# A three-stage transformer block on one core: the last stage's first row is normalised in attention buffers, its chunks start earlier, and VectorE takes more of the clamps

## The chip, the core and the metric

The kernel runs on one core of a Trainium2 chip. TensorE (PE) multiplies matrices and writes them to PSUM, VectorE (DVE) and ScalarE (ACT) work elementwise and can read PSUM, GpSimd (POOL) works on SBUF, and SyncE (SP) issues most of the DMAs. All DMAs that SP issues go through one queue, those of ACT through another. The metric is the device time of one execution in microseconds (us).

## What is computed

The input is 8 rows of 512 tokens by 512 numbers. Three stages follow each other, each with a residual:

```python
x = x + 0.5 * ffn(layernorm(x), w_gate_up, w_proj)      # stage a
x = x + attention(layernorm(x), Wq, Wk, Wv, Wo)          # stage b: 32 heads of 16, window 128
x = x + 0.5 * ffn(layernorm(x), w_gate_up, w_proj)      # stage c, the same weights

def ffn(x):                       # weights are ternary by groups of 64, times a group's scale
    gate, up = split(x @ quant(w_gate_up).T)             # 2 x 2048 columns
    h = silu(gate) * up
    return rms_norm(h) @ quant(w_proj).T                 # 2048 -> 512
```

## The kernel before, in words

**Feed-forward stages.** A row's 2048 hidden columns are 16 chunks of 128. To keep precision, what is multiplied is split in a high and a low term (`xs[:, 0]` and `xs[:, 1]`, `hs[:, 0]` and `hs[:, 1]`). One chunk (`chunk`, `gate_or_up`, L297) is 16 matmuls for gate and up, a silu on ACT, a product on DVE (L313) and squares on POOL for the norm (L583 to L587). The down projection of a chunk (`project`, L330) is 8 matmuls and needs both terms of h (high on ACT L318, low on DVE L322). A layernorm (`norm`) has three parts for each of a row's 4 blocks of 128 tokens: statistics (DVE, L206, L207), scaling (DVE, L219) and transposition (PE, L227, then ACT and, when split, DVE, L230 and L231). Tiles for weights of one chunk hold 512 KB and are loaded again in stage c from a copy in DRAM (`weights_loaded`, L255).

**Attention.** It goes in 128 units u: 8 rows times 4 groups of heads (i = u // 4) times 4 token blocks (t = u % 4). PE, DVE, ACT, POOL and SP all run in the order in which the loop issues work (`manual_schedule`), so a wait on one engine holds everything after it there. In unit u PE makes the transposed scores (`probabilities`, tile `sp`, L921), the weighted values of unit u-1 (`weighted`, `av`, L956), the scores for the maxima of unit u+6 (`maxima`, `sm`, L873), at t = 2 a small transposition (`neg`, L900), and then one filler of 8 matmuls (L797): values `wv` of the next row at t = 0, an output projection `wo` at t = 1, queries `wq` at t = 2 and keys `wk` at t = 3, both for i+3. The scores of a unit are clamped (ACT L933 for three of four groups, DVE L929 for one), go through an exponential (ACT L935) and two selects (POOL L940). Silu and the exponential need different ACT tables, and each change is an `ACT_TABLE_LOAD` of 1.28 us. Queries and keys are copied to a ring by SP's DMAs (L828, L840) out of the tiles `raw` (`q_31` and `k_31` are the last). The denominators go to DRAM and back (L979, L989), are inverted on DVE (`inverted`, L993, at t = 2 of the next group of units), stored (L994), spread by eight DMAs (L1001) and multiplied in by POOL (L1007), all in the order of the queue.

**The close.** From unit 116 on there are no more queries and keys, and from 112 on no values: fillers run out. The first row of stage c is therefore worked off beside the last units (`FirstRow`, called `row_c`). `closing` is unit 112. There the right-hand buffers of the attention's begin are freed (`right`: the x, normalised x and transposed x of row 0 and even rows, `wv`, and the values `vones0`), and stage c's own buffers are put there. The row's norm is made in units 113 to 116, chunk c in unit 117 + c, and its down projection in units 133 to 148. Chunk weights are loaded where buffers come free: chunk 0 at unit 112, chunks 1 to 8 at unit 116 (in place of `raw`, `wq`, `wk` and `xs1`), 9 to 11 at 120, 12 to 14 at 124, and 15 at 129, followed there by eight loads of the projection's weights (L639, 512 KB each). In memory, the tile of chunk 1's weights lies over the end of `q_31` and the first 1216 bytes (a partition) of `k_31`, and a load waits until all that read the old tiles under it are done. The products h of chunks 0 to 12 are stored to DRAM (L652) and read back (`back`, L658) for the down projection; those of the last KEPT = 3 stay. The output projections of row 7 come in units 138 to 141.

Places in the trace: a unit begins with the first `sp` matmul. Unit 112 begins at 1561.83 us, the keys of unit 115 (the last) end at 1593.62, unit 118 begins at 1612.42, unit 128 at 1685.20, and the chunks of stage c's second row begin at 1764.20. From there on PE works without a pause to the end.

The lines that place the norm, the chunks and the loads:

```python
closing, early = units - row, units - row + TB + 1
for u in range(-3 * TB, early + 2 * FC):
    if u == closing:
        right.close()
        row_c.opened(ps_s, ps_av, ps_mm)
        row_c.weights(range(1))
    if u == closing + TB:
        brought.close()
        row_c.weights(range(1, 9))
    ...
    if 0 <= u - early < FC:
        row_c.chunk(u - early)
    if 0 <= u - early - FC < FC:
        row_c.down(u - early - FC)
```

Of the kernel before, what the change touches and what calls it, by code (L numbers as in the profile page):

```python
# [24 lines left out]
def macaron_block(  # L25
# [166 lines left out]

    def norm(xnpool, xspool, psum, tag, xt, split, name, each=False):

        if split:
            xs = xspool.tile([P, 2, DC, T], F32R, tag="xs", name=f"xs_{name}")
        else:
            xs = xspool.tile([P, DC, T], F32, tag="xs", name=f"xs_{name}")  # L200
        mv = small.tile([P, TB, 2], F32, tag="mv", name=f"mv_{name}")
        rstd = small.tile([P, TB], F32, tag="nrstd", name=f"rstd_{name}")

        def statistics(t):
            st = small.tile([P, 6], F32, tag="st", name=f"st_{name}_{t}")
            nc.vector.bn_stats(st, xt[:, t, :])  # L206
            nc.vector.bn_aggr(mv[:, t, :], st)  # L207

            if each or t == TB - 1:
                which = slice(t if each else 0, t + 1)  # L210
                var = small.tile([P, TB], F32, tag="nvar", name=f"var_{name}_{t}")
                nc.vector.tensor_scalar(var[:, which], mv[:, which, 1], LN_EPS, None, ALU.add)
                inv_sqrt(rstd[:, which], var[:, which])

        xns = {}

        def scaled(t):
            xns[t] = xnpool.tile([P, D], F32, tag="xn", name=f"xn_{name}_{t}")
            nc.vector.tensor_scalar(  # L219
                xns[t], xt[:, t, :], mv[:, t, 0:1], rstd[:, t : t + 1], ALU.subtract, ALU.mult  # L220
            )

        def transposed(t):
            xn = xns.pop(t)
            pt = psum.tile([P, DC, P], F32, tag=tag, name=f"ptn_{name}_{t}")
            for c in range(DC):
                nc.tensor.transpose(pt[:, c, :], xn[:, c * P : (c + 1) * P], ident)  # L227
            cols = slice(t * P, (t + 1) * P)
            if split:
                nc.scalar.copy(xs[:, 0, :, cols], pt)  # L230
                nc.vector.tensor_tensor(  # L231
                    xs[:, 1, :, cols], pt, xs[:, 0, :, cols].bitcast(F32), ALU.subtract
                )
            else:
                nc.scalar.copy(xs[:, :, cols], pt)

        return xs, statistics, scaled, transposed
# [4 lines left out]
    def ffn_stage(kind, source, target, first):  # L242
# [27 lines left out]
        if first:  # L270
            xspools.append(pool(s, f"xs0_{kind}", 1))
# [4 lines left out]
            xspools.append(pool(s, f"xs1_{kind}", 1))  # L276
# [16 lines left out]
        def gate_or_up(b, c, i):  # L293
            ps = bank("mm", [P, T], f"gu_{kind}{b}_{c}_{i}")
            for k in range(DC):
                for part in range(2):
                    nc.tensor.matmul(  # L297
                        ps, wgu[c][:, i * DC + k, :], xss[b][:, part, k, :],
                        start=(k == 0 and part == 0), stop=(k == DC - 1 and part == 1),
                    )  # L300
# [309 lines left out]
        class FirstRow:  # L610


            KEPT = 3

            def opened(self, ps_s, ps_av, ps_mm):
                nonlocal xnpool, work
                banks["mm"] = banks["acc"] = banks["tr"] = ps_s, "s"
                banks["ms"] = ps_mm, "mm"
                self.ps_av = ps_av
                xspools.append(pool(s, f"xs0_{kind}", 1, side="right"))  # L620
                xpools.append(pool(s, f"x0_{kind}", 1, side="right"))
                xnpool = pool(s, f"xn_{kind}", 2, side="right")
                work = pool(s, f"work_{kind}", 5, side="right")
                self.kept, self.terms = {}, {}
                row_loaded(0)
                self.norm = norms[0]

            def weights(self, chunks):
                weights_made(pool(s, f"weights{chunks[0]}_{kind}", 1, side="right"), chunks)
                weights_loaded(chunks)  # L630

# [23 lines left out]
            def back(self, e):  # L655
                if e < FC - self.KEPT:
                    self.kept[e] = work_tile("back", 0, e)
                    nc.sync.dma_start(self.kept[e], h_kept[e])  # L658

            def down(self, n):  # L660
                order = [*range(FC - self.KEPT, FC), *range(FC - self.KEPT)]
                if n == 0:
                    self.ops = outputs(0)
                    banks["tr"] = self.ps_av, "av"
                    for e in range(self.KEPT):
                        self.back(e)
                if n >= 1 and n + 2 < FC:
                    ahead = order[n + 2]
                    self.terms[ahead] = high_term(0, ahead, self.kept[ahead])
                    low_term(self.kept.pop(ahead), self.terms[ahead])  # L670
                    self.back(ahead + self.KEPT)
                project(self.ops, order[n], self.terms.pop(order[n]), order[0], order[-1])
# [18 lines left out]
        def rest():  # L691
            xspools.append(pool(s, f"xs1_{kind}", 1))
            banks_opened()
# [9 lines left out]
    def attention_begun(step, ps_tr):  # L703

        at = 3
        if step == at:
# [4 lines left out]
            nc.sync.dma_start(xt, rows_a[0])  # L711
            begun["norm"] = norm(begun["xn"], begun["xs0"], *ps_tr, xt, False, "b0")
        for part, first_step in enumerate((at + 3, at + 8, at + 9)):
# [3 lines left out]
    def attention_stage(row_c):  # L717
# [11 lines left out]
        xpool, xnpool = begun["x"], begun["xn"]  # L729
        fixed = {name: pool(right, f"{name}_b", 1, side="right") for name in ("wv", "vones0")}  # L730
        fixed["wo"] = pool(base, "wo_b", 1)
# [9 lines left out]
        for name in ("wq", "wk"):  # L741
            fixed[name] = pool(brought, f"{name}_b", 1)
        xspools = [begun["xs0"], pool(brought, "xs1_b", 1)]

# [13 lines left out]
        for name, src in (("wq", wq_t), ("wk", wk_t), ("wv", wv_t), ("wo", wo_t)):  # L758
            attn_w[name] = fixed[name].tile([P, DC, D], F32, name=f"{name}_sb")
            if name != "wo":  # L760
# [39 lines left out]
        def project(w, b, j, done):  # L800
            cols = slice(j * P, (j + 1) * P)
            pairs = [(attn_w[w][:, k, cols], xss[b][:, k, :]) for k in range(DC)]
            sum_of_products(f"{w}_{b}_{j}", pairs, done)
# [40 lines left out]
        def values(b, t):  # L844
            rows = slice(t * P, (t + 1) * P)
            pairs = [(xss[b][:, k, rows], attn_w["wv"][:, k, :]) for k in range(DC)]

# [58 lines left out]
        def probabilities(u):  # L906
# [19 lines left out]
            for g in range(NG):  # L926
                under = pT[:, 2 * g : 2 * g + 2, : n * P]
                if g == 1:
                    nc.vector.tensor_scalar(  # L929
# [99 lines left out]
        }  # L1029
        s.enter_context(tc.manual_schedule(engines=engines))  # L1030
        outputs = {}
        for out_b in range(B):
            for out_t in range(TB):
                at = TB * (NJ * (out_b + 1) + 2 + out_t) + 1
                outputs[at if out_b < B - 1 else units + 2 * TB + 2 + out_t] = out_b, out_t
        closing, early = units - row, units - row + TB + 1
        for u in range(-3 * TB, early + 2 * FC):
            i, t = u // TB, u % TB
            b, j = i // NJ, i % NJ
            if u == closing:  # L1040
                right.close()
                row_c.opened(ps_s, ps_av, ps_mm)
                row_c.weights(range(1))
# [6 lines left out]
            if u == closing + 3 * TB:  # L1050
                rings[0].close()
                row_c.weights(range(12, 15))
            if u == units + 1:
                scores.close()
                row_c.weights(range(15, FC))
                row_c.down_opened()
            if 0 <= u < units:
                probabilities(u)
# [55 lines left out]
        base.close()  # L1114

    ffn_stage("a", lambda b: tokens(x, b), lambda b: rows_a[b], True)
    row_c, rest = ffn_stage("c", lambda b: rows_b[b], lambda b: tokens(out, b), False)
    attention_stage(row_c)
    rest()


# [26 lines left out]
```

## Time and profile before

| | us |
|---|---|
| median of 3 runs | 2405.08 |
| lowest, highest | 2404.55, 2410.36 |
| the profiled execution: its own time | 2405.92 |
| its span | 2404.2 |
| PE busy in the span | 2333.5 (97%) |
| the close, unit 112 to the second row's chunks (1561.83 to 1764.20) | 202.4 |
| of it PE busy | 188.1 |

The profiled execution is 1.7 us longer than its span (what lies around it) and 0.8 us above the median. A line of the timeline gives the start, the duration, engine, line of code, operation, output and inputs, and how often it came in a row; in brackets stands how long the engine had been idle and whom it waited for. "PEclk" or the column PEclk is the granted TensorE clock as a share of full speed. SPq and ACTq are DMA issues; their duration is that of the issuing, not of the transfer.

### The profile page before, as it was taken

Reading aid. Unit: us, or ns where it says so; the run is one execution under the profiler, and the core shown is the slowest. Engines: PE = TensorE matmul, PEld = TensorE weight load, DVE = VectorE, ACT = ScalarE, POOL = GpSimd, SP = SyncE. Lnnn points to the kernel's source line nnn. Section 1 sums busy time; section 2 is a strip of 40 time slices with the busy share of each in tenths; the row PEclk is TensorE's granted clock in tenths of the full one; section 3 lists DMA queues with packets and bytes.
Section 4 is the critical chain, followed back from the end, with each engine's and each line's share of the span. In section 5 each row is a group of like instructions: output and inputs, shape, how many; then the busy total and the mean of one; then the engine's idle time right before and its main releaser. Section 6 shows DMA issues by size and latency. Waiting matters only on the chain.

```text
span 2404.2 us, 42982 instructions
## 1 busy us (share of the span) xinstructions
PE 2333.5 (97%) x16824; PEld 1721.1 (72%) x16824; DVE 1301.7 (54%) x3673; ACT 987.0 (41%) x1432; POOL 902.4 (38%) x746
## 2 busy tenths in 40 slices
PE   5999999999999999999999999989999999999998
PEld 4778888888888555555555555556688888888886
DVE  7884544444543566767667676663254444444443
ACT  6773222222222156655666666558222222222221
POOL 0000345444445223433333333335334544544544
PEclk9899999999999999999999999989999999999999
DMA  4443200000001334344444443453610010010000
GB/s 163 143 150 135 84 20 16 35 19 17 36 35 36 105 71 113 87 125 121 110 127 108 118 113 104 102 181 125 211 62 18 18 36 18 18 36 18 18 18 18
DMA packets 89995, 185.78 MB, mean 77 GB/s; under 512 B 22464, under 2 KB 26560, under 8 KB 86720
## 3 DMA queue, kind: packets, MB, share of 16 engines
q1 hardware_dynamic: 74480, 141.87, 20.9%
q10 hardware_dynamic: 15312, 41.16, 4.6%
q8 instruction: 132, 2.16, 0.4%
q14 instruction: 71, 0.58, 0.1%
HBM read 78.64 MB, written 45.61 MB: 52 GB/s over the span
## 4 chain that ended last, share of the span: by engine, by line
PE 88%; DVE 4%; ACT 3%; DMA 2%; issue 1%; POOL 1%; SPq 0%; ACTq 0%; POOLq 0%; DVEq 0%
PE gu_c L297 18%; PE gu_a L297 18%; PE o_c L330 9%; PE o_a L330 9%; PE wv L797 5%; PE wq L797 5%; PE wk L797 5%; PE wo L797 5%; PE av L956 4%; PE sp L921 4%; PE sm L873 4%; PE neg L900 1%; ACT pT L935 1%; PE ptn_a L227 1%; PE ptn_b L227 1%
## 5 line engine op out<-in xcount | busy, mean ns | idle before, releaser
L297 PE MATMUL gu_a<-xs_a,wgu_a 128*128 128x512 f32 x2048 | 497.0, 396 | 8.0 <-ACT sg_a L308 3.0
L297 PE MATMUL gu_c<-xs_c,wgu_c 128*128 128x512 f32 x2048 | 491.9, 393 | 0.4 <-ACT sg_c L308 0.4
L297 PEld LDWEIGHTS gu_a<-xs_a,wgu_a 128*128 128x128 f32 x2048 | 385.6, 190 | 91.3 <-ACT sg_a L308 4.3
L940 POOL TENSOR_SCALAR_AFFINE_SELECT pT<-pT 128x1024 f32<-128x1024 f32 x224 | 243.2, 1106 | 528.9 <-ACT pT L935 524.8
L297 PEld LDWEIGHTS gu_c<-xs_c,wgu_c 128*128 128x128 f32 x2048 | 381.8, 188 | 83.2 <-issue 2.3
L881 DVE CUSTOM_DVE_ANT_0 seen<-sm,window 128x256 f32<-128x256 f32 (+1 forms) x1024 | 331.4, 387 | 84.2 <-PE sm L873 83.5
L330 PE MATMUL o_c<-wp_c,hs_c 128*128 128x512 f32 x1024 | 256.8, 395 | 4.1 <-ACT hs_c L318 3.5
L330 PE MATMUL o_a<-wp_a,hs_a 128*128 128x512 f32 x1024 | 257.1, 396 | 1.6 <-DVE hs_a L322 1.6
L313 DVE TENSOR_TENSOR h_c<-gu_c,sg_c 128x512 f32<-128x512 f32 x128 | 88.3, 690 | 287.6 <-PE gu_c L297 251.6
L586 POOL TENSOR_TENSOR sq_c<-h_c 128x512 f32<-128x512 f32 x120 | 125.1, 1042 | 302.1 <-DVE h_c L313 290.9
L933 ACT ACTIVATE pT<-sp 128x512 f32<-128x512 f32 (+1 forms) x384 | 181.2, 545 | 134.7 <-PE sp L921 134.7
L330 PEld LDWEIGHTS o_c<-wp_c,hs_c 128*128 128x128 f32 x1024 | 192.8, 189 | 48.5 <-ACT hs_c L318 4.0
L330 PEld LDWEIGHTS o_a<-wp_a,hs_a 128*128 128x128 f32 x1024 | 193.0, 190 | 42.0 <-DVE hs_a L322 2.5
L935 ACT ACTIVATE pT<-pT 128x2048 f32<-128x2048 f32 (+1 forms) x128 | 217.4, 1699 | 8.4 <-DVE neg_terms L891 3.1
L313 DVE TENSOR_TENSOR h_a<-gu_a,sg_a 128x512 f32<-128x512 f32 x128 | 88.3, 690 | 231.1 <-PE gu_a L297 226.4
L587 POOL TENSOR_TENSOR ss_c<-ss_c,sq_c 128x512 f32<-128x512 f32 x120 | 188.7, 1573 | 9.0
L586 POOL TENSOR_TENSOR sq_a<-h_a 128x512 f32<-128x512 f32 x90 | 94.2, 1047 | 225.2 <-DVE h_a L313 214.5
L308 ACT ACTIVATE sg_c<-gu_c 128x512 f32<-128x512 f32 x128 | 76.6, 598 | 248.7 <-PE gu_c L297 239.0
L318 ACT CAST hs_c<-h_c 128x512 fp32r<-128x512 f32 x115 | 71.4, 621 | 233.6 <-DVE h_c L313 233.6
L308 ACT ACTIVATE sg_a<-gu_a 128x512 f32<-128x512 f32 x128 | 76.4, 597 | 206.3 <-PE gu_a L297 201.9
L318 ACT CAST hs_a<-h_a 128x512 fp32r<-128x512 f32 x115 | 71.4, 620 | 207.5 <-DVE h_a L313 205.1
L322 DVE TENSOR_TENSOR hs_c<-h_c,hs_c 128x512 fp32r<-128x512 f32 x115 | 112.7, 980 | 75.0 <-ACT hs_c L318 75.0
(134 smaller groups left out, 3023.1 us busy)
## 6 DMA issues: line engine op xcount, KB each, us to landing
ks<-k SPq DMA_DIRECT2D x128, 256.0 KB
qs<-q SPq DMA_DIRECT2D x128, 128.0 KB
wf_gu<-w_gate_up_dram SPq DMA_DIRECT2D x16, 512.0 KB
wgu_kept<-wgu_a ACTq DMA_DIRECT2D x16, 512.0 KB
rows_a<-x_a ACTq DMA_DIRECT2D x8, 1024.0 KB
x_b<-rows_a SPq DMA_DIRECT2D x8, 1024.0 KB
oT<-sums SPq DMA_DIRECT2D x64, 128.0 KB
rep<-inverses SPq DMA_DIRECT2D x256, 32.0 KB
```

What stands on the lines that cost most here:

```text
L297: nc.tensor.matmul(ps, wgu[c][:, i * DC + k, :], xss[b][:, part, k, :], start=(k == 0 and part == 0), stop=(k == DC - 1 and part == 1),)
L308: nc.scalar.activation(sg, gate, AF.Silu)
L313: nc.vector.tensor_tensor(h, up, sg, ALU.mult)
L318: nc.scalar.copy(hs[:, 0, :], h)
L330: nc.tensor.matmul(ops[t], hs[:, part, t * P : (t + 1) * P], wp[e // 2][:, e % 2, :], start=(e == begin and part == 0), stop=(e == end and ...
L586: nc.gpsimd.tensor_tensor(sq, h, h, ALU.mult)
L587: nc.gpsimd.tensor_tensor(sumsq, sumsq, sq, ALU.add)
L797: nc.tensor.matmul(ps, lhs, rhs, start=(n == 0), stop=(n == len(pairs) - 1))
L881: nc.vector.tensor_tensor_reduce(out=seen[:, : n * P], in0=tiles[g][:, h, : n * P], in1=window[:, (2 - n) * P :], scale=-1.0, scalar=3.4e3 ...
L933: nc.scalar.activation(under, tiles[g][:, :, : n * P], AF.Relu, scale=-1.0)
L935: nc.scalar.activation(seen, seen, AF.Exp, scale=-1.0)
L940: nc.gpsimd.affine_select(out=half, in_=half, compare_op=ALU.is_ge, fill=0.0, base=0, pattern=[[0, 2 * NG], [sign, P]], channel_multiplier ...
```

## The change

- The norm of stage c's row 0 moves from units 113 to 116 to the attention's row 6: the row is loaded at unit 96, statistics are made at units 98, 100, 102 and 104, scaling at 107 to 110, transposition at 108 to 111. It uses the attention's x buffer, its normalised-x buffers, and for the two terms the buffers of `xs0` and `wv`, which are therefore kept to the very end; at unit 112 only `vones0` is freed, for the work tiles and chunk 0's weights.
- Chunk 0 moves from unit 117 to 113, chunk c (1 to 15) from 117 + c to 115 + c. The output projection that was in unit 113 goes to 112. The down projection goes from units 133 to 148 to units 131 to 146.
- Chunk weights are loaded two a unit instead of all at once where their buffers come free. Chunk 1's load stays in unit 116, where now chunk 1 is too. Chunk 15's stays in unit 129.
- KEPT is 2 instead of 3, so chunk 13's product too goes to DRAM and back. The first three reads back are issued in units 129, 130 and 131 instead of all in the first down step, and the high and low terms are made two steps ahead from the first step on.
- In the last six units, 122 to 127, DVE makes the clamps of three groups and ACT that of one.

```diff
-    def norm(xnpool, xspool, psum, tag, xt, split, name, each=False):
-        if split:
-            xs = xspool.tile([P, 2, DC, T], F32R, tag="xs", name=f"xs_{name}")
-        else:
-            xs = xspool.tile([P, DC, T], F32, tag="xs", name=f"xs_{name}")
+    def norm(xnpool, xspools, psum, tag, xt, split, name, each=False):
+        xs = [
+            p.tile([P, DC, T], F32R if split else F32, tag="xs", name=f"xs{n}_{name}")
+            for n, p in enumerate(xspools)
+        ]
...
         class FirstRow:
-            KEPT = 3
-            def opened(self, ps_s, ps_av, ps_mm):
-                nonlocal xnpool, work
+            KEPT = 2
+            def opened(self, ps_s, ps_av, ps_mm, xpool, xn, terms):
+                nonlocal xnpool
...
-                xspools.append(pool(s, f"xs0_{kind}", 1, side="right"))
-                xpools.append(pool(s, f"x0_{kind}", 1, side="right"))
-                xnpool = pool(s, f"xn_{kind}", 2, side="right")
-                work = pool(s, f"work_{kind}", 5, side="right")
+                xspools.append(terms)
+                xpools.append(xpool)
+                xnpool = xn
                 self.kept, self.terms = {}, {}
                 row_loaded(0)
                 self.norm = norms[0]
+                self.coming = []
+
+            def working(self):
+                nonlocal work
+                work = pool(s, f"work_{kind}", 5, side="right")
 
             def weights(self, chunks):
                 weights_made(pool(s, f"weights{chunks[0]}_{kind}", 1, side="right"), chunks)
-                weights_loaded(chunks)
+                self.coming += chunks
+
+            def load(self):
+                if self.coming:
+                    weights_loaded([self.coming.pop(0)])
...
                 if n == 0:
                     self.ops = outputs(0)
                     banks["tr"] = self.ps_av, "av"
-                    for e in range(self.KEPT):
-                        self.back(e)
-                if n >= 1 and n + 2 < FC:
-                    ahead = order[n + 2]
-                    self.terms[ahead] = high_term(0, ahead, self.kept[ahead])
-                    low_term(self.kept.pop(ahead), self.terms[ahead])
-                    self.back(ahead + self.KEPT)
+                if n + 2 < FC:
+                    self.terms[n] = high_term(0, n, self.kept[n])
+                    low_term(self.kept.pop(n), self.terms[n])
+                    self.back(n + 3)
...
-                if g == 1:
+                if g == 1 or (g > 1 and u >= units - AHEAD):
                     nc.vector.tensor_scalar(
                         under, tiles[g][:, :, : n * P], -1.0, 0.0, ALU.mult, ALU.max
                     )
...
+        closing = units - row
...
                 at = TB * (NJ * (out_b + 1) + 2 + out_t) + 1
+                if at == closing + 1:
+                    at = closing
                 outputs[at if out_b < B - 1 else units + 2 * TB + 2 + out_t] = out_b, out_t
-        closing, early = units - row, units - row + TB + 1
-        for u in range(-3 * TB, early + 2 * FC):
+        chunk_at = {closing + 1: 0, **{closing + TB + c: c + 1 for c in range(FC - 1)}}
+        down_at = closing + TB + FC - 1
+        for u in range(-3 * TB, down_at + FC):
+            if u == closing - row:
+                row_c.opened(ps_s, ps_av, ps_mm, xpool, xnpool, [begun["xs0"], fixed["wv"]])
             if u == closing:
-                right.close()
-                row_c.opened(ps_s, ps_av, ps_mm)
+                first_values.close()
+                row_c.working()
                 row_c.weights(range(1))
...
             if u == closing + 3 * TB:
                 rings[0].close()
-                row_c.weights(range(12, 15))
+                row_c.weights(range(12, FC - 1))
             if u == units + 1:
                 scores.close()
-                row_c.weights(range(15, FC))
+                row_c.weights(range(FC - 1, FC))
+                row_c.load()
                 row_c.down_opened()
+            if closing <= u < units:
+                row_c.load()
+                row_c.load()
...
-            for part, first in enumerate((1, 2, 3)):
+            for part, first_step in enumerate((closing - row + 2, closing - 5, closing - 4)):
                 for block in range(TB):
-                    if u == closing + first + (0 if part == 0 else block // 2):
+                    if u == first_step + block * (2 if part == 0 else 1):
                         row_c.norm[part](block)
-            if 0 <= u - early < FC:
-                row_c.chunk(u - early)
-            if 0 <= u - early - FC < FC:
-                row_c.down(u - early - FC)
+            if down_at - 2 <= u < down_at + 1:
+                row_c.back(u - down_at + 2)
+            if u in chunk_at:
+                row_c.chunk(chunk_at[u])
+            if u >= down_at:
+                row_c.down(u - down_at)
```

More of the change, by code (lines that the diff above doesn't have):

```diff
@@ L229, in transposed @@
             if split:
-                nc.scalar.copy(xs[:, 0, :, cols], pt)
+                nc.scalar.copy(xs[0][:, :, cols], pt)
                 nc.vector.tensor_tensor(
-                    xs[:, 1, :, cols], pt, xs[:, 0, :, cols].bitcast(F32), ALU.subtract
+                    xs[1][:, :, cols], pt, xs[0][:, :, cols].bitcast(F32), ALU.subtract
                 )
             else:
-                nc.scalar.copy(xs[:, :, cols], pt)
+                nc.scalar.copy(xs[0][:, :, cols], pt)
         return xs, statistics, scaled, transposed
@@ L270, in ffn_stage @@
         if first:
-            xspools.append(pool(s, f"xs0_{kind}", 1))
+            xspools.append(2 * [pool(s, f"xs0_{kind}", 2)])
             xpools += 2 * [pool(s, f"x_{kind}", 2)]
@@ L275, in ffn_stage @@
             weights_made(pool(s, f"weights1_{kind}", 1), range(EARLY, FC))
-            xspools.append(pool(s, f"xs1_{kind}", 1))
+            xspools.append(2 * [pool(s, f"xs1_{kind}", 2)])
             projection_made(pool(s, f"weights2_{kind}", 1))
@@ L297, in gate_or_up @@
                     nc.tensor.matmul(
-                        ps, wgu[c][:, i * DC + k, :], xss[b][:, part, k, :],
+                        ps, wgu[c][:, i * DC + k, :], xss[b][part][:, k, :],
                         start=(k == 0 and part == 0), stop=(k == DC - 1 and part == 1),
@@ L655, in back @@
             def back(self, e):
-                if e < FC - self.KEPT:
+                if e < FC - self.KEPT and e not in self.kept:
                     self.kept[e] = work_tile("back", 0, e)
@@ L691, in rest @@
         def rest():
-            xspools.append(pool(s, f"xs1_{kind}", 1))
+            xspools.append(2 * [pool(s, f"xs1_{kind}", 2)])
             banks_opened()
@@ L711, in attention_begun @@
             nc.sync.dma_start(xt, rows_a[0])
-            begun["norm"] = norm(begun["xn"], begun["xs0"], *ps_tr, xt, False, "b0")
+            begun["norm"] = norm(begun["xn"], [begun["xs0"]], *ps_tr, xt, False, "b0")
         for part, first_step in enumerate((at + 3, at + 8, at + 9)):
@@ L729, in attention_stage @@
         xpool, xnpool = begun["x"], begun["xn"]
-        fixed = {name: pool(right, f"{name}_b", 1, side="right") for name in ("wv", "vones0")}
+        first_values = ExitStack()
+        fixed = {"wv": pool(right, "wv_b", 1, side="right")}
+        fixed["vones0"] = pool(first_values, "vones0_b", 1, side="right")
         fixed["wo"] = pool(base, "wo_b", 1)
@@ L742, in attention_stage @@
             fixed[name] = pool(brought, f"{name}_b", 1)
-        xspools = [begun["xs0"], pool(brought, "xs1_b", 1)]
+        xspools = [[begun["xs0"]], [pool(brought, "xs1_b", 1)]]
         s = ExitStack()
@@ L758, in attention_stage @@
         for name, src in (("wq", wq_t), ("wk", wk_t), ("wv", wv_t), ("wo", wo_t)):
-            attn_w[name] = fixed[name].tile([P, DC, D], F32, name=f"{name}_sb")
+            attn_w[name] = fixed[name].tile([P, DC, D], F32, tag="xs", name=f"{name}_sb")
             if name != "wo":
@@ L801, in project @@
             cols = slice(j * P, (j + 1) * P)
-            pairs = [(attn_w[w][:, k, cols], xss[b][:, k, :]) for k in range(DC)]
+            pairs = [(attn_w[w][:, k, cols], xss[b][0][:, k, :]) for k in range(DC)]
             sum_of_products(f"{w}_{b}_{j}", pairs, done)
@@ L845, in values @@
             rows = slice(t * P, (t + 1) * P)
-            pairs = [(xss[b][:, k, rows], attn_w["wv"][:, k, :]) for k in range(DC)]
+            pairs = [(xss[b][0][:, k, rows], attn_w["wv"][:, k, :]) for k in range(DC)]
             def kept(ps):
@@ L1114, in attention_stage @@
         base.close()
+        return right
     ffn_stage("a", lambda b: tokens(x, b), lambda b: rows_a[b], True)
     row_c, rest = ffn_stage("c", lambda b: rows_b[b], lambda b: tokens(out, b), False)
-    attention_stage(row_c)
+    right = attention_stage(row_c)
     rest()
+    right.close()
 def kernel(L0_attn_x, L0_attn_Wq, L0_attn_Wk, L0_attn_Wv, L0_attn_Wo, L0_ffn_w_gate_up, L0_ffn_w_proj):
```

## The prediction

> **What bounds the kernel now.** I read the page's busy times and slices first, then a table by stages, then the timelines of PE, SP, DVE and ACT in the close, and last the waits of the DMA queue.
>
> The page: PE is busy 97% of the span, so only its idle or slow time can be won. Between start and end one slice alone falls short in PE and in clock, the 27th (1563 to 1623), where the close begins.
>
> ```profile
> PE 2333.5 (97%) x16824; PEld 1721.1 (72%) x16824; DVE 1301.7 (54%) x3673; ACT 987.0 (41%) x1432; POOL 902.4 (38%) x746
> PE   5999999999999999999999999989999999999998
> PEclk9899999999999999999999999989999999999999
> ```
>
> Stages (from:to, length, busy PE, PEld, DVE, ACT, POOL, clock, DMA share, GB/s): the attention before the close, units 112 to 115, 116 and 117, 118 to 127, and the rest of the close. In the first PE has no pause. Then 4.6, 1.3, 3.8 and 4.5 us are idle, and the granted clock falls to 0.84 and 0.91.
>
> ```profile
> 1541.00:1561.83 20.83, 20.83 (x233) 11.52 (x231) 13.38 (x68) 11.17 (x17) 8.75 (x8) 1.00 0.41 112
> 1561.83:1593.62 31.79, 27.18 (x303) 15.86 (x303) 19.56 (x87) 15.08 (x21) 9.74 (x9) 0.84 0.48 136
> 1593.62:1612.42 18.80, 17.46 (x169) 11.61 (x167) 11.60 (x42) 11.87 (x16) 4.27 (x4) 0.91 0.75 240
> 1612.42:1685.20 72.78, 68.95 (x777) 50.84 (x776) 27.74 (x97) 63.49 (x76) 43.20 (x39) 1.00 0.40 136
> 1685.20:1764.20 79.00, 74.51 (x314) 52.30 (x314) 28.62 (x49) 16.91 (x28) 20.07 (x17) 0.98 0.54 176
> ```
>
> PE's timeline: what follows a pause is slow. The same eight matmuls of 512 columns take 3.60 us at full clock, 6.05 after a pause of 2.73, and the projection's 8 take 3.83 after 3.53, where 32 in a row take 7.70, or 1.925 for 8.
>
> ```profile
> 1579.71 1.09 PE L900 MATMUL neg<-ident,neg_terms 128*128 128x128 f32 x4 [2.73 <-DVE neg_terms L892]
> 1580.59 6.05 PE L797 MATMUL wq<-xs_b,wq_sb 128*128 128x512 f32 x8
> 1708.53 3.60 PE L797 MATMUL wo<-wo_sb,oT 128*128 128x512 f32 x8
> 1716.65 1.88 PE L330 MATMUL o_c<-wp_c,hs_c 128*128 128x512 f32 x7 [0.61 <-DVE hs_c L322]
> 1722.06 3.83 PE L330 MATMUL o_c<-wp_c,hs_c 128*128 128x512 f32 x8 [3.53 <-ACT hs_c L318]
> ```
>
> SP's timeline and its wait: the copies of the last keys are issued to 1598.20, and the first weights load over their source waits 4.8 us for them to land. Later, one weights load and eight of the projection stand in the queue ahead of the denominators' way back.
>
> ```profile
> 1595.06 3.14 SPq L840 DMA_DIRECT2D ks<-k  x4
> 1603.12 4.19 SPq L255 DMA_DIRECT2D wgu_c<-wgu_kept  x8
> 1693.40 0.35 SPq L255 DMA_DIRECT2D wgu_c<-wgu_kept  x1
> 1693.86 4.63 SPq L639 DMA_DIRECT2D wp_c<-wp_kept  x8
> 1699.03 0.32 SPq L989 DMA_DIRECT2D den<-dens  x1
> 1717.65 3.26 SPq L658 DMA_DIRECT2D back_c<-h_kept  x5
> ```
> ```profile
> SPq L255 <- DMA ks<-k: 4.8, 1, 4.8
> ```
>
> DVE and ACT: the reciprocal holds DVE until those denominators land at 1708.6, and with it three products; the read back holds ACT.
>
> ```profile
> 1708.65 0.35 DVE L993 RECIPROCAL inv<-den 128x32 f32<-128x32 f32 x1 [10.05 <-DMA den<-dens]
> 1708.92 0.63 DVE L313 TENSOR_TENSOR h_c<-gu_c,sg_c 128x512 f32<-128x512 f32 x1
> 1710.23 0.98 DVE L322 TENSOR_TENSOR hs_c<-h_c,hs_c 128x512 fp32r<-128x512 f32 x1 [0.69 <-ACT hs_c L318]
> 1721.39 1.97 ACT L318 CAST hs_c<-back_c 128x512 fp32r<-128x512 f32 x3 [6.24 <-DMA back_c<-h_kept]
> ```
>
> **The change, part by part**, as differences to the profiled execution (2405.92, that is 1.7 around its span and 0.8 above the median); the sum is then put on the median.
>
> *Units 96 to 111: +2.4.* The x load (1 MB) goes to a queue that rows up to 7 have used the same way. Statistics and scaling find the places that the earlier rows' norms had, where PE had no pause: 0. The four transpositions are PE work, 0.35 each between starts (1755.04 to 1755.39): +1.4. New beside them is DVE's subtraction of 0.69 at the end of units 108 to 111; it holds the next clamp, and with it a PSUM bank that PE's `sm` needs. In units 116 and 117 such holds cost 0.23 and 0.25; DVE is fuller here. Between 0 and 0.5 each; I take 0.25: +1.0.
>
> *Units 112 to 115: -2.15.* Now 31.79. With fillers in each unit they would take what units 108 to 111 take, 6.38 + 6.15 + 6.57 + 6.14 up to 0.1, or 25.35: the pile of four statistics that made the 2.73 pause is gone, and the output projection and chunk 0 (about 3.75 for 16 matmuls, as 3.70 for 8 unsplit ones) fill 112 and 113. But chunk 0's weights are issued only behind the copies of the keys, 4.65 into unit 112, and share their queue: 1 MB at the some 200 GB/s that the DMA rows of half a microsecond show there ends near 7.5, and 512 KB at the 400 of the loads at 1607 to 1613 near 8.8. A read of 256 KB took 3.74 from issue to use (1717.65 to 1721.39), 0.65 of it data, so some 2.4 follow the data: landed at 11.2, wanted at 6.4 + 2.55 = 8.95. Wait 2.2 (0 to 3.5). After a short thin stretch at 1565 a filler took 5.03 instead of 3.63, so +1.4 slow (0 to 2.5). The changes of ACT's table and DVE's product cost some 0.7, as in unit 119 (7.43 for 6.2 of work, half of that here). 25.35 + 2.2 + 1.4 + 0.7 = 29.65.
>
> *Units 116 and 117: +11.4.* Now 18.80 from the end of the last keys. The step that decides: chunk 1 stands in unit 116, 2.9 after the keys (`sp`, `av`, `sm`). Its weights lie over the source of the keys' copies, as before, because the right-hand buffers are 44 KB a partition at unit 116 in both kernels. The copies land 9.4 after the keys (1603.0), the load issues at 9.5, and lands at least 256 KB more at 400 GB/s than the 3.74 above, so 4.4 later: 13.9. PE waits 11.0, and everything that it feeds waits behind it (SP too: the store of h 1 stands ahead of loads 3 and 4, which are wanted a unit later, so nothing more). Bounds: 8.5 if the load is as quick as the store of 256 KB (2.06), 12 if two loads share. Then chunk 1, 3.75, slow by the row 6.05 - 3.60 = 2.45; then unit 117 with output and chunk, between 9.1 and 11.2 (units 125 and 121), 10.1. Sum 13.9 + 3.75 + 2.45 + 10.1 = 30.2.
>
> The page on the DMA of the Trainium skill ("DMA: Bandwidth & Descriptors", Rules for kernel authors) says to issue a load early and wait for it late, and it speaks against this placement; its fit of about 2 us plus size over 436 GB/s would land 512 KB in 3.2 and make the sum 1.2 smaller. No run here shows that fit alone.
>
> *Units 118 to 127: -0.5.* The same work in the same places, two chunks further. Three clamps on DVE (0.60 between starts) instead of three on ACT (1.57): the exponential starts at 1647.3 instead of 1648.26 in unit 122 and similarly after, which can remove the pauses of 0.26 and 0.35 for `pT` and `sg`; the maxima's split stands 1.2 later on DVE in unit 122, but its second cast of 1.25 ended with a POOL operation at 1647.84 and does so still: +0.25. Bounds -1.5 to +1.5.
>
> *From unit 128: -3.4.* Now 79.0. Count from its start, 1685.20. Chunk 13 ends at 5.35, as chunk 11 now. Output to 8.4, chunk 14 to 12.1, chunk 15 to 15.9 (its load, issued at 8.2, lands near 12.6, inside the next wait), first projection to 17.8. Chunk 15's product stands behind the reciprocal in DVE's order, and the queue ahead of that is what it was: the denominators land at 23.4, and the terms are there 2.6 later, as at 1711.2. So the second projection waits from 17.8 to 26.0, where before three chunks and an output covered most of it: 8.2 (6 to 10). It then ends at 26.0 + 1.9 + 1.9 slow = 29.8. The rest is work: output 3.03, 14 projections at 1.925, sums 0.8, four outputs with 5.28 for a pair instead of 4.95, transpositions 1.4, together 45.3, plus 0.5 that the same count misses today: 75.6. The earlier reads back remove today's 3.53; they are used 3 us or more after they land.
>
> Sum: 2.4 - 2.15 + 11.4 - 0.5 - 3.4 = **+7.75**, on the median 2405.08 + 7.75 = **2412.8**.
>
> "TensorE: Matmul & The Clock Gate" of the Trainium skill (Part 1) has the clock at half after an idle window of 3.4 us until a busy one has passed. By it the two long waits would each cost 1.7 to 3.4 afterwards, where I take 2.45 and 1.9 from the rows, and the 2.2 wait for chunk 0 nothing.
>
> **The rivals.**
> - *Chunk 1's weights come in time.* For it: the transfer itself is 1.3 us, and no row shows this load being waited for. Against it: the 4.8 us wait of SP. Price: -11.0 - 2.45, so 2399.4, not slower. It decides below a wait of about 4 us.
> - *DVE does not hold chunk 15* (denominators land some 8 us sooner, because eight loads drain faster or start later). For it: only the order in the queue holds them. Against: 400 GB/s is steady to 1708. Price -8.2 - 1.9: 2402.7, the same.
> - *Both*: the plan works as drawn, 7.75 - 13.45 - 10.1 = -15.8, 2389.3.
> - *More slow clock and more holds*: chunk 0's wait at 3.5 and its slow stretch 2.5, holds of 0.5 in four units, 12 for chunk 1 and 10 for chunk 15: +1.3 + 1.1 + 1.0 + 1.0 + 1.8 more, 2419.0, and up to 2424 if the clamps cost their 1.5 and the slow stretches last twice as long.
> - *The clamps change nothing, or the bound moves to ACT*: inside the 1.5 above.
>
> **How the numbers follow.** A difference of 0.3% (7.2 us) is about what a measurement of this kernel can tell from none. The computed case has 0.60, with its own range 2406 to 2418, and its centre lies just past the bound: 0.40 slower, 0.20 same. Weights in time 0.08 (0.03 faster, 0.05 same); no hold on chunk 15 0.06 (same); both 0.12 (faster); more waits 0.14 (slower). Faster 0.15, same 0.31, slower 0.54. The range of 2393 to 2423 leaves about a tenth below, in the case of both, and a tenth above.
>
> **What would show it.** Right: a first `gu_c` at unit 113 and a pause of about 11 us on PE ahead of the second chunk, with SP waiting for `ks` just before; a clock below 0.9 behind it; a pause near 8 us between the first and second projection with DVE's reciprocal waiting for `den`; no 2.73 pause for `neg` at unit 114. Wrong: chunk 1 starting within 4 us of its scores, or the projections running through. The prediction fails most easily in the landing of two loads, which no row times alone.

## The result and the profile after

The changed kernel takes 2415.51 us (median of 10 runs, 2410.64 to 2423.19) where the kernel before takes 2405.49 (10 runs): the ratio is 1.0039, with a 95% interval of 1.0021 to 1.0056. It is slower by 10 us, where 7.75 were forecast. The profiled execution of the changed kernel took 2419.9 with a span of 2418.2; it lies 4.4 above its median. Of this, 0.7 to 3.0 stand in units 112 to 115, which take 29.39 here and 26.4 to 28.7 in the five other profiles of the experiments that leave this stage as it is. The rest was not traced; the time ahead of unit 98, where all these kernels do the same work but for one load at unit 96, also differs between profiled executions (unit 98 begins at 1466.14 at the earliest and at 1473.40 at the latest, 1473.40 before and 1473.36 after the change).

The page of the changed kernel: PE has the same work, 2333.8 us, in a longer span. Slices 27 and 29 (1572 to 1632 and 1693 to 1753 us), both in the close, now fall short, at 7 and 8 tenths.

```profile
PE 2333.8 (97%) x16824; PEld 1721.3 (71%) x16824; DVE 1308.4 (54%) x3685; ACT 987.3 (41%) x1424; POOL 902.6 (37%) x746
PE   5999999999999999999999999979899999999998
PEclk9999999999999989999999999989999999999999
```

By stages (from:to, length, then the busy time of PE, PEld, DVE, ACT and POOL, the granted clock, DMA share and GB/s): units 98 to 111, 112 to 115, 116 and 117, 118 to 121, 122 to 127, and from unit 128 to the second row's chunks.

```profile
1473.36:1567.75 94.39, 92.58 (x1105) 54.47 (x1105) 63.64 (x291) 54.33 (x78) 32.35 (x30) 1.00 0.39 101
1567.75:1597.14 29.39, 27.25 (x317) 17.28 (x316) 17.02 (x78) 18.38 (x25) 9.79 (x9) 0.94 0.44 111
1597.14:1625.63 28.49, 18.36 (x170) 13.08 (x170) 9.05 (x37) 13.09 (x15) 6.58 (x6) 0.82 0.52 156
1625.63:1657.56 31.93, 29.95 (x349) 22.02 (x349) 18.09 (x78) 26.22 (x31) 18.09 (x16) 1.00 0.54 183
1657.56:1701.96 44.40, 39.99 (x429) 29.70 (x429) 15.71 (x31) 31.73 (x33) 26.02 (x23) 0.96 0.31 99
1701.96:1778.30 76.34, 68.17 (x281) 46.81 (x281) 27.39 (x47) 16.43 (x27) 16.12 (x13) 0.93 0.56 183
```

Against the same stages before, the lengths in the two profiled executions are given below. The keys are taken to end where the next matmul starts (1593.51 in the kernel before, where the prediction has 1593.62), so 31.68 and 18.91 stand for the prediction's 31.79 and 18.80.

| stage | before | after | difference | forecast |
|---|---|---|---|---|
| units 98 to 111 | 88.43 | 94.39 | +6.0 | +2.4 |
| units 112 to 115, to the end of the last keys | 31.68 | 29.39 | -2.3 | -2.15 |
| units 116 and 117 | 18.91 | 28.49 | +9.6 | +11.4 |
| units 118 to 127 | 72.78 | 76.33 | +3.6 | -0.5 |
| from unit 128 | 79.0 | 76.34 | -2.7 | -3.4 |
| sum | 290.8 | 304.94 | +14.1 | +7.75 |

PE's timeline of the changed kernel shows the two long waits that the forecast rests on: 10.13 us ahead of chunk 1 (11.0 forecast) and 6.95 + 0.22 between the first and the second projection (8.2 forecast). The first line is chunk 0, the third and fourth are unit 122, where a pause of 2.15 is followed by a chunk at 5.38 instead of 3.9.

```profile
1578.87 5.50 PE L297 MATMUL gu_c<-xs_c,wgu_c 128*128 128x512 f32 x16 [2.01 <-ACT pT L942]
1610.09 5.79 PE L297 MATMUL gu_c<-xs_c,wgu_c 128*128 128x512 f32 x16 [10.13 <-DMA wgu_c<-wgu_kept]
1661.70 0.90 PE L907 MATMUL neg<-ident,neg_terms 128*128 128x128 f32 x4 [2.15 <-DVE neg_terms L899]
1662.24 5.38 PE L297 MATMUL gu_c<-xs_c,wgu_c 128*128 128x512 f32 x16
1727.66 0.79 PE L330 MATMUL o_c<-wp_c,hs_c 128*128 128x512 f32 x1 [6.95 <-ACT hs_c L318]
1728.68 3.36 PE L330 MATMUL o_c<-wp_c,hs_c 128*128 128x512 f32 x7 [0.22 <-DVE hs_c L322]
```

SP's timeline has what lies behind them. The load of chunks 1 and 2 is issued 9.09 us after the last keys' matmuls (1597.14), behind the copies of those keys, and chunk 1 starts 3.86 after it. SP's waits say what held it: the copies' landing, twice, 3.4 at the longest. The denominators' way back stands behind one chunk's weights and eight loads of the projection, and DVE's reciprocal waits for it until 1726.06, with chunk 15's product behind.

```profile
1598.60 3.27 SPq L847 DMA_DIRECT2D ks<-k  x4
1606.23 0.80 SPq L255 DMA_DIRECT2D wgu_c<-wgu_kept  x2
1710.79 0.37 SPq L255 DMA_DIRECT2D wgu_c<-wgu_kept  x1
1711.60 5.05 SPq L647 DMA_DIRECT2D wp_c<-wp_kept  x8
1716.69 0.56 SPq L996 DMA_DIRECT2D den<-dens  x1
```
```profile
SPq L255 <- DMA ks<-k: 4.2, 2, 3.4
```
```profile
1726.06 0.35 DVE L1000 RECIPROCAL inv<-den 128x32 f32<-128x32 f32 x1 [8.35 <-DMA den<-dens]
1726.33 0.63 DVE L313 TENSOR_TENSOR h_c<-gu_c,sg_c 128x512 f32<-128x512 f32 x1
```

Two losses had not been forecast. In the units from 98 on, DVE's timeline has the statistics between the last copy of one unit (`q`) and the first clamp of the next, and PE's scores for the maxima wait for that clamp. (Of the 6.0 lost in these units PE stands idle for 1.8. The rest is busy time, 92.58 instead of 88.43, with the four transpositions in it.)

```profile
1480.66 0.69 DVE L818 SCALAR_TENSOR_TENSOR q<-wq,q 128x512 fp32r<-128x512 f32 x1 [2.59 <-ACT q L817]
1481.27 0.68 DVE L206 BATCH_NORM_STATS2 st_c<-x_c 128x6 f32<-128x512 f32 x1
1481.99 0.18 DVE L207 BATCH_NORM_AGGREGATE mv_c<-st_c 128x2 f32<-128x6 f32 x1
1482.09 0.41 DVE L936 TENSOR_SCALAR pT<-sp 128x256 f32<-128x256 f32 x1
```
```profile
1482.55 0.74 PE L880 MATMUL sm<-ks,qs 32*128 32x256 f32 x13 [0.41 <-DVE pT L936]
```

And in units 122 to 127 ACT's timeline has the change of its table, 1.28 us, not beside DVE's clamps but behind them, so that the exponential starts 1.29 later than the clamps would allow, and 3.29 after ScalarE's first clamp began, where the kernel before has 2.88 (1645.38 to 1648.26):

```profile
1658.56 0.60 ACT L940 ACTIVATE pT<-sp 128x512 f32<-128x512 f32 x1 [0.77 <-PE sp L928]
1660.56 1.28 ACT L942 ACT_TABLE_LOAD   x1 [1.40 <-DVE pT L936]
1661.85 1.91 ACT L942 ACTIVATE pT<-pT 128x2048 f32<-128x2048 f32 x1
```

### The profile page after: what moved, and what is told of

Read it like the earlier page. It is cut to its first block, busy times and chain, and to the rows that moved or that the text cites. A ratio compares the mean times of both kernels' runs of the same rounds, so it can differ in the third digit from the quotient of the medians.

```text
span 2418.2 us, 42974 instructions
## 1 busy us (share of the span) xinstructions
PE 2333.8 (97%) x16824; PEld 1721.3 (71%) x16824; DVE 1308.4 (54%) x3685; ACT 987.3 (41%) x1424; POOL 902.6 (37%) x746
## 4 chain that ended last, share of the span: by engine, by line
PE 90%; DVE 5%; ACT 2%; issue 1%; DMA 1%; POOL 0%; SPq 0%; ACTq 0%; POOLq 0%; DVEq 0%
PE gu_c L297 19%; PE gu_a L297 17%; PE o_c L330 9%; PE o_a L330 9%; PE wv L804 5%; PE wo L804 5%; PE wq L804 5%; PE wk L804 5%; PE av L963 4%; PE sp L928 4%; PE sm L880 4%; PE neg L907 1%; ACT pT L942 1%; PE ptn_a L227 1%; PE ptn_c L227 1%
## 5 line engine op out<-in xcount | busy, mean ns | idle before, releaser
L297 PE MATMUL gu_c<-xs_c,wgu_c 128*128 128x512 f32 x2048 | 497.5, 396 | 12.5 <-DMA wgu_c<-wgu_kept 10.1
L940 ACT ACTIVATE pT<-sp 128x512 f32<-128x512 f32 x372 | 176.2, 545 | 132.2 <-PE sp L928 132.2
```

The source lines that it names most:

```text
L297: nc.tensor.matmul(ps, wgu[c][:, i * DC + k, :], xss[b][part][:, k, :], start=(k == 0 and part == 0), stop=(k == DC - 1 and part == 1),)
L940: nc.scalar.activation(under, tiles[g][:, :, : n * P], AF.Relu, scale=-1.0)
```

## The experiments

Single runs of these kernels scatter by 10 us and more, so two things are given for each: the ratio to the kernel before on the same chip, with its interval, where there are several runs of both; and the length of the stage that the edit touches, which repeats to 0.1 us between the profiles of different kernels where the edit does not touch it and no slow stretch falls in it (units 118 to 121 take 31.86 to 31.93 in the changed kernel and all that derive from it).

### The clamps, undone and alone

```diff
-                if g == 1 or (g > 1 and u >= units - AHEAD):
+                if g == 1:
```

> The changed kernel with one part undone: ScalarE again makes three of the four clamps in units 122 to 127. Theory: the table load of 1.28 us, which in the trace of the changed kernel stands idle behind VectorE's clamps (1.40 to 2.11 us), goes back to follow ScalarE's own clamps, and units 122 to 128 lose the pauses for av (0.97, 0.94, 1.00): 2 to 4.5 us faster than the changed kernel, 2411 to 2413.5. Rival (the clamps cost nothing, the pauses come from the two more chunks beside these units): within 1 us of the changed kernel, 2414.5 to 2416.5.

Measured: ratio 1.0016 (1.0005 to 1.0027) where the changed kernel has 1.0039. Units 122 to 127 are 3.6 shorter than in the changed kernel, as the theory has it, and take what they take before, 40.79; PE's pauses for `av` there come to 0.3:

```profile
1653.84:1694.63 40.79, 38.30 (x429) 28.45 (x428) 10.62 (x19) 37.37 (x46) 26.41 (x24) 1.00 0.34 107
```

The same edit the other way round, on the kernel before:

> The kernel before with the clamps alone changed (VectorE makes three of four in the last six units), nothing else. Theory: 2 to 4 us slower than before, 2407.5 to 2409.5, with ScalarE's table loads in units 122 to 127 idle behind VectorE. Rival, and the step of the prediction: 0.5 faster, 1.5 either way, 2404 to 2407.

Measured: ratio 1.0004 (0.9989 to 1.0019), which settles nothing. The stage does: units 122 to 127 take 44.29 instead of 40.82, and the trace has the table load idle behind DVE (1.40 in unit 122, the second line) with the old norm and the old place of the chunks.

```profile
1639.76:1684.05 44.29, 39.93 (x429) 29.76 (x428) 15.70 (x31) 31.67 (x33) 26.03 (x23) 0.96 0.29 99
```
```profile
1642.75 1.28 ACT L935 ACT_TABLE_LOAD   x1 [1.40 <-DVE pT L929]
```

The clamps cost some 3.5 us in these units in both kernels, of which about 1.3 is a slow stretch behind the pause of 2.15 that not every execution has (the same stage takes 43.12 in the run with early weights, without one). The pause for `neg` is 2.14 or 2.15 in all seven profiles with VectorE's clamps, and six of them have the slow chunk behind it; it is 1.88 in the three with ScalarE's clamps (before, clamps undone, all together), and none has. In unit 128 the clamps cost 0.6 more (the pause for `av` is 1.00 in the changed kernel and 0.37 with the clamps undone).

### The table loaded beside the clamps

```diff
-    nc.scalar.activation(const.tile([P, 1], F32, name="begin"), ones, AF.Silu)
+    begin = const.tile([P, 1], F32, name="begin")
+    nc.scalar.activation(begin, ones, AF.Silu)
...
+            if u >= units - AHEAD:
+                nc.scalar.activation(begin, ones, AF.Exp)
             seen = pT[:, :, : n * P]
```

> The changed kernel with VectorE's clamps kept, and a one-column exponential on ScalarE ahead of the wait for them in units 122 to 127, so that the table is loaded while VectorE works. It adds six instructions of about 0.2 us whose result nobody reads. Theory: unit 122 to 128 takes 40 to 41.5 us instead of 44.4 (40.8 with the clamps undone). Rival (VectorE's own 1.9 us for three clamps behind the product is what is late): 43 or more.

Measured: 41.74, a hair outside the theory's range and far from the rival's; one slow chunk (5.50 behind `neg`) is in it. In ACT's timeline of this run the load follows ACT's own clamp at once, and the exponential starts 2.02 after that clamp began where the changed kernel needs 3.29:

```profile
1654.26 0.60 ACT L941 ACTIVATE pT<-sp 128x512 f32<-128x512 f32 x1 [0.77 <-PE sp L929]
1654.88 1.28 ACT L943 ACT_TABLE_LOAD   x1
1656.17 0.20 ACT L943 ACTIVATE begin<-ones 128x1 f32<-128x1 f32 x1
1656.28 1.90 ACT L945 ACTIVATE pT<-pT 128x2048 f32<-128x2048 f32 x1
```

So most of the clamps' cost, 2.7 of 3.6, is the place of the table load, not DVE's time for them. Without the slow chunk (5.50, where the same 16 matmuls take 3.91 at full clock) the stage would take some 40.2, an estimate from this one execution: 0.6 less than with ScalarE's clamps, about what the forecast had expected of the clamps.

### Chunk 1's weights ahead of the keys' copies

```diff
-        xspools = [[begun["xs0"]], [pool(brought, "xs1_b", 1)]]
+        last_x = ExitStack()
+        xspools = [[begun["xs0"]], [pool(last_x, "xs1_b", 1)]]
...
         def keys_kept(i, ps):
+            if i == B * NJ - 1:
+                last_x.close()
+                row_c.weights(range(1, 3))
+                row_c.load()
+                row_c.load()
...
-                row_c.weights(range(1, 9))
+                row_c.weights(range(3, 9))
```

> The changed kernel with the weights of chunks 1 and 2 laid over the transposed x of row 7, whose last reader is the last keys' matmuls, and loaded right behind those, ahead of the copies of the keys on SyncE's queue. Nothing else. Theory: the 10.1 us wait ahead of chunk 1 shrinks to 0 to 2 us and the slow 5.79 behind it to about 3.9: 9 to 12 us faster than the changed kernel, 2403.5 to 2406.5. Rival (the wait is only the first of several in that place: another transfer or engine is late next, or the delayed copies hold the scores): less than 4 us faster, 2411.5 or more.

Measured: 2402.17, ratio 0.998 (0.9963 to 0.9997), so 0.6% below the changed kernel and, alone among the four single edits that have an interval, faster than before, if only just. Units 116 and 117 take 17.78 instead of 28.49, at full clock. In PE's timeline chunk 1 waits 1.34 and runs at its normal pace; in SP's the load is issued 0.1 after the last keys:

```profile
1588.24:1606.02 17.78, 16.43 (x171) 11.67 (x170) 9.05 (x37) 13.10 (x15) 6.58 (x6) 1.00 0.70 216
```
```profile
1592.41 3.87 PE L297 MATMUL gu_c<-xs_c,wgu_c 128*128 128x512 f32 x16 [1.34 <-DMA wgu_c<-wgu_kept]
```
```profile
1588.34 0.80 SPq L255 DMA_DIRECT2D wgu_c<-wgu_kept  x2
1589.70 4.43 SPq L853 DMA_DIRECT2D ks<-k  x4
```

The wait for chunk 1 with the slow stretch behind it is 10.7 us, the largest single cost of the change, and nothing took its place. The edit moves the load in the queue and in memory at once; which of the two would do alone was not tried.

### The denominators ahead of the loads

```diff
                 scores.close()
+                denominators_back(B * NJ - 1)
...
-                if t == 1:
+                if t == 1 and u != units + 1:
                     denominators_back(i - 1)
```

> The changed kernel with one DMA moved: the last denominators are read back ahead of the nine weights loads of unit 129 instead of behind them. Theory: VectorE's reciprocal no longer waits 8.35 us and chunk 15's terms are there when the second projection comes, so the pause of 6.95 goes; what is late next is the first read back, which still stands behind the loads, 2 to 4 us: 3 to 6 us faster than the changed kernel, 2409.5 to 2412.5. Rival (the projection's weights themselves are what it would wait for next): within 1.5 us of the changed kernel.

Measured: ratio 1.0015 (1.0002 to 1.0029), 0.24% below the changed kernel. From unit 128 it takes 71.36 instead of 76.34. The reciprocal no longer waits, the second projection waits 0.51, and what is late next is, as expected, the first read back, for 1.32 (2 to 4 expected):

```profile
1714.27 0.34 DVE L1000 RECIPROCAL inv<-den 128x32 f32<-128x32 f32 x1
1718.53 1.89 PE L330 MATMUL o_c<-wp_c,hs_c 128*128 128x512 f32 x7 [0.51 <-DVE hs_c L322]
1725.18 0.50 PE L330 MATMUL o_c<-wp_c,hs_c 128*128 128x512 f32 x1 [1.32 <-ACT hs_c L318]
```

### The statistics earlier in their units

The calls for statistics and scaling go to the place in the loop where the attention's own norms are called, ahead of values, queries and keys:

```diff
                 norms[b + 2][j - 1](t)
+            for block in range(TB):
+                if u == closing - row + 2 + 2 * block:
+                    row_c.norm[0](block)
+                if u == closing - 5 + block:
+                    row_c.norm[1](block)
...
-            for part, first_step in enumerate((closing - row + 2, closing - 5, closing - 4)):
-                for block in range(TB):
-                    if u == first_step + block * (2 if part == 0 else 1):
-                        row_c.norm[part](block)
+            for block in range(TB):
+                if u == closing - 4 + block:
+                    row_c.norm[2](block)
```

> The changed kernel with statistics and scaling of the moved norm issued earlier within the same units: behind the reciprocal and ahead of the unit's values, queries and keys, where the attention's own rows have theirs, instead of at the unit's end. Nothing else. Theory: what unit 98 to 108 lost (65.9 us for 63.2 before) is VectorE's order, 0.87 us of statistics standing between the last copy of a unit and the first clamp of the next; it goes: unit 98 to 112 takes 91.4 to 92.0 us instead of 94.4. Rival (VectorE is simply full in these units, wherever the work stands): 94 to 94.5.

Measured in one run (2410.87, against 2408.4 for the kernel before on that chip): units 98 to 111 take 90.68 instead of 94.39, better than expected, since the scaling's place had also delayed units 108 to 111. PE has no wait left there that the profile lists. What stays, 2.25 over before, is almost all the four transpositions' own time: each takes 0.53 from its start to that of the next scores (1546.89 to 1547.42), 2.1 in all.

```profile
1470.66:1561.34 90.68, 90.62 (x1105) 53.76 (x1104) 64.81 (x291) 54.30 (x78) 33.01 (x30) 1.00 0.40 105
```

### Chunk 0's weights a unit earlier

```diff
-            if u == closing:
+            if u == closing - 1:
                 first_values.close()
                 row_c.working()
                 row_c.weights(range(1))
+                row_c.load()
```

> The changed kernel with chunk 0's weights loaded at the start of unit 111 instead of 112, ahead of the copies of the keys that are issued at the end of 111. Nothing else. Theory: the wait of 2.01 ahead of chunk 0 and what is slow behind it (5.50 for 3.75) go: unit 112 to the end of the last keys takes 25.3 to 26.2 us instead of 29.4. Rival (the wait was only in part the weights): 27 or more.

Measured in one run (2412.12): units 112 to 115 take 25.76 instead of 29.39, and chunk 0 follows its unit's scores without a wait:

```profile
1573.49 3.92 PE L297 MATMUL gu_c<-xs_c,wgu_c 128*128 128x512 f32 x16
```

In the changed kernel's timeline the wait of 2.01 is put down to ScalarE's exponential (`pT`), which ended just then. It was the weights: here chunk 0 begins at 1573.49, before the same exponential does (1573.64). In the other runs that keep the late load the stage takes 26.4 to 28.7 with waits of 0.63 to 1.29 ahead of chunk 0, so of the 3.6 about 1 is the wait as it usually is, and the rest a longer wait in that one execution and its slow stretch.

### All together

The clamps undone, the weights of chunks 0 to 2 early, the denominators first and the statistics at their earlier place, all by the edits above; and the projection's first read back issued by hand behind two of its loads:

```diff
-                for u in [*range(n, FC // 2), *range(n)]:
+                for at, u in enumerate([*range(n, FC // 2), *range(n)]):
                     nc.sync.dma_start(wp[u].bitcast(F32), wp_kept[u])
+                    if at == 1:
+                        self.back(0)
...
-            if down_at - 2 <= u < down_at + 1:
+            if down_at - 2 < u < down_at + 1:
```

> The changed kernel with all that the runs point to: clamps undone, chunks 1 and 2 loaded ahead of the copies of the last keys, chunk 0 a unit earlier, statistics and scaling ahead in their units, the last denominators ahead of the loads of unit 129, and the first read back behind the second of the projection's loads instead of behind all eight. Theory: the gains add up, stage by stage 92 + 26 + 17.5 + 31.9 + 40.8 + 70 = 278 us from unit 98 to the second row's chunks, where before takes 290.8: 0.4 to 0.6% faster than before. Rival (a wait that each part alone hid comes out when the others go): less than 0.25% faster than before.

Measured: 2393.14, ratio 0.9941 (0.9919 to 0.9962): 0.6% faster than before, 1% faster than the change as it was made. The stages, in the order of the table above, come to 277.76 us where 278 were expected and the kernel before takes 290.8:

```profile
1466.14:1556.84 90.70, 90.64 (x1106) 53.74 (x1106) 64.82 (x291) 54.32 (x78) 32.94 (x30) 1.00 0.39 105
1556.84:1582.60 25.76, 25.64 (x317) 16.17 (x316) 17.11 (x78) 18.40 (x25) 9.79 (x9) 1.00 0.47 129
1582.60:1600.54 17.94, 16.46 (x169) 11.66 (x168) 9.05 (x37) 13.09 (x15) 6.59 (x6) 1.00 0.67 219
1600.54:1632.47 31.93, 29.95 (x349) 22.02 (x349) 18.16 (x78) 26.22 (x31) 18.09 (x16) 1.00 0.59 200
1632.47:1673.26 40.79, 38.30 (x429) 28.45 (x428) 10.62 (x19) 37.37 (x46) 26.41 (x24) 1.00 0.32 107
1673.26:1743.90 70.64, 66.70 (x282) 45.25 (x282) 27.39 (x47) 15.82 (x26) 15.21 (x13) 1.00 0.58 198
```

Each stage takes what the single edits gave it, and the clock is 1.00 in all six. The profiled execution, 2385.46, lies 7.7 below the median; it is 7.3 earlier than the kernel before already at unit 98, ahead of all that was changed but one load, so only the stages are compared.

One wait did come out in the last stage, and it belongs to the edit that had not been tried alone. With the read back issued by hand the first one is in time, but the projection of the next waits 1.83 and the one behind it 0.71, where the run with the denominators first waited 1.32 at the first and not again:

```profile
1701.41 0.50 PE L330 MATMUL o_c<-wp_c,hs_c 128*128 128x512 f32 x1 [1.83 <-ACT hs_c L318]
1705.51 0.51 PE L330 MATMUL o_c<-wp_c,hs_c 128*128 128x512 f32 x1 [0.71 <-ACT hs_c L318]
```

The stage is 0.7 shorter all the same, with the clock at 1.00 where that run has 0.98; that moving the read back gains anything is not shown.

## Why the prediction was right

It was right in direction, in size (7.75 forecast, 10 measured) and in its two main steps, the waits of some 10 and 7 us. It was wrong in two terms: the holds of units 98 to 111 and the clamps. That the size fits is in part luck: by the table these two are 7.6 too small together, the other three terms come out 1.2 too large, and the profiled executions differ by 14, the medians by 10.

- *Chunk 1's weights.* Right: SP waited for the copies as before, PE for the weights. The wait was 10.13, not 11.0: the issue came 9.1 after the keys and not 9.5, and 512 KB were there 3.86 after it and not 4.4. The early load shows the whole cost. (The fit that the prediction takes from "DMA: Bandwidth & Descriptors" is given there for DMAs that GpSimd issues, and these are SP's; 3.86 here and 4.07 with the early load lie between its 3.2 and the forecast's 4.4.)
- *Chunk 15 behind the reciprocal.* Right in mechanism; 7.2 instead of 8.2, and 71.36 instead of 76.34 when the denominators go first. (With four pairs at 5.28, as the prediction says, its work is 45.6 and not 45.3; PE's rows have 5.28 for three.)
- *Units 112 to 115.* -2.3 for -2.15. The pause of 2.73 for `neg` is gone, as forecast. The wait for chunk 0, 2.2 forecast, was 2.01 here and 0.63 to 1.29 in the other runs, where the stage takes 0.7 to 3.0 less, so that the number was met in this execution is luck. The 2.4 that the forecast lets follow the data is not worked out: 3.74 less 0.65 is 3.1, and no run times it alone.
- *Units 98 to 111.* Too small: the step "statistics and scaling find the places that the earlier rows' norms had ... 0" failed. They have the same units' spare time, but another place in the order: at the end of a unit, behind the last copy and ahead of the next clamp. Moving them within the units gave 3.7 of the 6.0 back. The 2.25 that stay are near the forecast's 2.4, but by other parts: the transpositions take 2.1 and not 1.4, and the holds by the subtraction, forecast at 1.0, are no more than what is left, 0.1.
- *The clamps.* Wrong in sign: the step "the exponential starts at 1647.3 instead of 1648.26" let the table load run beside DVE's clamps. It waits for them, since it belongs to the exponential that does. Forecast -0.5, measured +3.6 in units 118 to 127, all of it gone with the clamps undone. The +0.25 at the maxima's split did come (a pause of 2.15 for 1.88), and with it, in six of seven executions, a slow chunk.
- *Slow clock behind pauses.* The forecast took 1.4, 2.45 and 1.9 from rows; the changed kernel's execution had 1.6 behind chunk 0's wait (5.50 for 3.87), 1.9 in chunk 1 (5.79 for 3.87), and 1.7 and 0.9 in the projection and output behind the long wait, 2.6 together; one more, 1.5 in unit 122, was not foreseen. The two long waits fit the 1.7 to 3.4 that the prediction worked out from the Trainium skill; chunk 0's, which by that rule cost nothing, does not.

Of the excess over the forecast, 6.4 in the profiled executions (14.1 against 7.75), two thirds are gone in the medians (10). Units 112 to 115, shorter in the five other profiles, can account for 0.7 to 3.0 of that; for the rest the cause stays open, since only profiled executions show their stages.

## What to carry to other kernels

Work that was brought forward to fill an idle engine gained nothing here until its inputs came forward too: ask of the first moved step which transfer it now meets, what that transfer stands behind in its queue and in its memory, and move that with it. With an order written out by hand, spare time in a unit was not enough: the statistics had to stand ahead of the unit's last wait, not behind it, where they delayed the next unit's first clamp. And when work is taken from one engine to shorten a chain, look at what that engine did just behind it in the chain: here a table load that had been hidden became the chain.

## What the runs showed of the hardware

- In these runs a table load takes on the wait of the activation that it serves: in every one of the last six units the load of 1.28 us began only behind VectorE's clamps, after 0.81 to 2.11 us of idle time, until a one-column exponential of 0.20 us ahead of the wait took the load along.
- The same pause does not always make TensorE slow. Ahead of unit 122's chunk PE waited 2.14 us in the run with early weights (first two lines) and 2.15 with the early table load (last two); the chunk then took 3.91 at a granted clock of 1.00, and 5.50 at 0.69. It was slow in six of the seven executions with a pause of 2.14 or 2.15, and in none of three with 1.88; but at chunk 0 it took 5.50 behind 1.29 us and 3.87 behind 1.17.

```profile
1642.08 0.63 PE L913 MATMUL neg<-ident,neg_terms 128*128 128x128 f32 x4 [2.14 <-DVE neg_terms L905]
1642.46 3.91 PE L297 MATMUL gu_c<-xs_c,wgu_c 128*128 128x512 f32 x16
1657.41 0.63 PE L908 MATMUL neg<-ident,neg_terms 128*128 128x128 f32 x4 [2.15 <-DVE neg_terms L900]
1657.79 5.50 PE L298 MATMUL gu_c<-xs_c,wgu_c 128*128 128x512 f32 x16
```

The Trainium skill ("TensorE: Matmul & The Clock Gate", Part 1) describes a window of some 3.4 us that runs freely, that is, does not start anew with the kernel. That a pause's place in this window decides is not stated there and not shown here; it would agree with the scatter. The page also has the clock fall after an idle window, and pauses of 1.3 and 2.15 us are shorter than one; here the measured stretches decide. With no wait above 1.9 us the clock was 1.00 in all six stages of the last run's close.
